# A two-layer graph network on one Trainium2 core: the last pair's first tile is summed on VectorE too, in a buffer of its own, with a new order of the last steps

## The chip, the cores and the metric

The kernel runs on one core of a Trainium2 chip. The metric is the device time of one execution in microseconds (us). TensorE is called PE here, VectorE DVE, ScalarE ACT, GpSimd POOL and SyncE SP; SP does nothing but issue DMAs.

## The reference, cut to what matters

The input x holds 128 graphs of 64 nodes with 768 features (8192 rows, fp32), adj their 64 x 64 adjacency. Two layers follow each other; each one is a layer norm, a relu, a graph layer and a residual sum. Layer 0 is a convolution over the relations of the edges. Layer 1 is an attention over each graph with 6 heads of 128 features. For one graph, in short:

```python
h1 = relu(layernorm(hh))                 # hh = x + layer 0
H  = h1 @ W + b                          # 64 x 768: six heads of 128
G  = h1 @ H_w + H_b                      # the gate's input, 64 x 768
t  = tanh(H)
l[i, j, head] = leaky(t[i] . w_src + t[j] . w_dst)   # masked by adj
A  = softmax(l over j)                   # 64 x 64 for each head
f  = elu(A @ H + b)                      # 64 x 768
out = hh + sigmoid(G) * (f - h1) + h1    # gate between f and h1, then the residual
```

The kernel uses tanh for the sigmoid: sigmoid(G) = (1 + tanh(G / 2)) / 2.

## The kernel before, in words

**Tiles and passes.** Two graphs make a tile of 128 rows: NT = 64 tiles, taken in NP = 32 pairs. Pass 1 (to L1038) computes layer 0 and writes hh + h1 into the output tensor in DRAM, and the operands of layer 1 into DRAM scratch. Pass 2 (L1041 on) computes layer 1 pair by pair and adds its result to the output tensor. This text is about the last some 50 us of pass 2.

**The products.** H and G of a pair come from 15 products of block sums (PRODUCTS, L54). The steps P, R, RA and Ff issue a product (L1121), its reading into the tiles `hz` by DVE or ACT, and an operand sum on POOL or DVE. In the last pair a product is split into its H half and its G half (PH and PG, `whole_product`, L1377), read by RH, RAH (ACT) and RG (`read_one`, L1388).

**One tile's attention.** With the names that the order uses:

- `th` (tanh, ACT, L1159), `mul` (DVE, L1163), four `sum` steps (twelve accumulating ACT operations, L1173), `k` and `chain` (POOL, L1176 to L1186), `rows` (PE, L1206), `rrow` (DVE, L1210) and `lrow` (ACT, L1215), `log` (PE, L1225), `cp` (masking, DVE, L1229), `pre` (leaky, ACT, L1234), `tr` (largest of a row, DVE, L1238), `exp` (six ACT operations, L1246), `rec` (1 / sum, DVE, L1250).
- The weights are turned for PE. All pairs but the last do it by `tv` (DVE, L1267), `ts` (four stores to DRAM, L1272) and `tl` (a load of 192 KB into `pT`, L1278). The last pair does it by `turnp` (PE, L1256) and `pT` (ACT, L1261).
- `swap` (L1192): two DMAs that put one graph's features on the other graph's partitions, into `hx`, of which there are two buffers. `att` (PE, L1286) needs pT, hz and hx.
- `ev` (`divide`, DVE, three operations each for an even and an odd half of the heads, L1322) writes the result `f`. `e` (ACT, L1333) is its exponential, `g` (ACT, L1329) the gate, `lx` (SP, L1061) the load of h1, scaled in pass 1.
- `f` (`final`, DVE, three operations of 128 x 768, L1340, L1342, L1344), then `dma` (`store`, L1347): a DMA issued by POOL that adds 384 KB of f to the output tensor.

**The last pair's end.** Here e, f and the stores are split by the parity of the heads: `exp_part` (L1417), `final_part` (L1422, L1424, L1426, L1428) and `store_part` (L1430). Tiles in SUMMED_HERE get their old output loaded beside their h1 (`load_out`, L1409, 384 KB, tile `xo`), the sum is a fourth DVE operation (L1428), and SP stores the half plainly (L1433). Other tiles are added to the output by POOL (L1435).

**What sets the order.** The steps of pass 2 are written out by hand: ORDER, which a loop runs for each pair (L1466), and END (L115 to L147, run from L1473) for the last pairs. "name/k" is the step of the k-th pair before the last; without "/k" it is the last pair's; the digit behind a name is the tile in its pair (0 or 1), and the digits behind points are parts. Every engine runs its own instructions in this order (`manual_schedule`, L1458), so an instruction that waits holds up all behind it on its engine. I write f0.2/1 for the step so named, and NT-2 and NT-1 for the last pair's tiles 0 and 1.

**Buffers.** `f` comes from the pool `work` with two buffers, so tile t waits for the store of tile t-2. `xo` comes from the pool `keep`, tag "x", six buffers.

**Fillers.** For tile NT-1 alone `keep_awake` (L1194) issues 9 matmuls ahead of `rows` and 12 ahead of `log` whose result is overwritten (L1198).

Of the kernel before, what the change touches and what calls it, by code (L numbers as in the profile page):

```python
# [8 lines left out]
F32 = mybir.dt.float32  # L9
# [6 lines left out]
P = 128  # L16
# [96 lines left out]


END = """  # L115
g0/3 R1/2 R2/2 R14/3 Ff6/2 P3.1/2 Ff1/1 P11.0/2 R3/2 RA1/2 P4.0/2 rows0/3 P4.1/2 tv1/4 P6.0/2 th1/3
Ff11/2 rrow0/3 R4/2 lrow0/3 mul1/3 Ff4/1 sum1.2/3 P6.1/2 lx0/4 dma0/5 P7.0/2 rec0/4 sum1.1/3
sum1.0/3 P7.1/2 P8.0/2 log0/3 R6/2 Ff2/1 Ff8/1 Ff3/1 Ff7/1 Ff9/1 ts1/4 R7/2 swap0/4 P8.1/2 P9.0/2
k1/3 sum1.3/3 tl1/4 RA7/2 P9.1/2 Ff5/1 chain1/3 P11.1/2 R8/2 g1/3 P10.0/2 rows1/3 cp0/3 Ff10/1
pre0/3 P10.1/2 lrow1/3 R9/2 tr0/3 R11/2 memset1/3 th0/2 tl0/4 rrow1/3 att/4 log1/3 P12.0/2 P12.1/2  # L120
R10/2 P13.0/2 lx1/4 P13.1/2 mul0/2 exp0.0/3 ev1.0/4 ev1.1/4 sum0.3/2 ev0.0/4 ev0.1/4 e1/4 e0/4
sum0.2/2 P5.0/1 memset0/2 R12/2 g0/2 f1.0/4 cp1/3 P2.0/1 g1/4 P0.0/1 exp0.1/3 Ff6/1 swap1/3 f1.1/4
P14.0/2 P0.1/1 R13/2 pre1/3 f0.0/4 P14.1/2 sum0.0/2 f1.2/4 P1.0/1 f0.1/4 P2.1/1 R0/1 sum0.1/2 f0.2/4
RA0/1 RA2/1 R14/2 P1.1/1 RA1/1 P5.1/1 ld/1 P3.0/1 Ff11/1 R2/1 tr1/3 RA14/2 R1/1 RA5/1 R5/1 th1/2
tv0/3 mul1/2 exp1.0/3 P3.1/1 P8.0/1 Ff1 P8.1/1 exp1.1/3 k0/2 P4.0/1 dma0/4 chain0/2 tv1/3 ts0/3
sum1.1/2 rows0/2 rrow0/2 R3/1 sum1.2/2 lx1/3 P4.1/1 Ff2 Ff4 P11.0/1 lrow0/2 Ff5 P6.0/1 sum1.0/2
sum1.3/2 log0/2 P6.1/1 R4/1 k1/2 P7.0/1 cp0/2 Ff8 pre0/2 R6/1 P7.1/1 tr0/2 P9.0/1 exp0.0/2 ts1/3
R8/1 dma1/4 Ff3 P9.1/1 memset1/2 Ff9 rec0/3 R7/1 Ff10 Ff7 exp0.1/2 tv0/2 chain1/2 tl0/3 rows1/2
RA7/1 lrow1/2 P11.1/1 rrow1/2 lx0/3 P10.0/1 log1/2 swap0/3 tl1/3 R9/1 rec1/3 P10.1/1 R11/1 cp1/2
R10/1 th0/1 att/3 pre1/2 P13.0/1 mul0/1 sum0.3/1 ev1.1/3 ev0.0/3 memset0/1 sum0.1/1 sum0.2/1  # L130
sum0.0/1 lx0/2 ev1.0/3 ts0/2 ev0.1/3 P13.1/1 k0/1 P12.0/1 P12.1/1 tr1/2 chain0/1 R13/1 swap1/2 PH2
swap0/2 e1/3 R12/1 e0/3 PH0 P14.0/1 P14.1/1 f1.0/3 f0.0/3 f1.1/3 exp1.0/2 R14/1 exp1.1/2 tv1/2 PH5
f1.2/3 rows0/1 f0.1/3 RA14/1 lrow0/1 RAH0 dma1/3 f0.2/3 PH1 PG0 PH3 ts1/2 th1/1 RAH5 RAH1 RAH2
mul1/1 PH11 dma0/3 tl0/2 PH4 RH3 lx1/2 memset1/1 Ff6 sum1.0/1 RH4 Ff11 tl1/2 sum1.1/1 PH6 rrow0/1
PH7 RH6 sum1.3/1 RAH7 log0/1 PH9 RG0 sum1.2/1 cp0/1 RH9 pre0/1 rec0/2 RH11 PH8 RH8 PH10 th0 k1/1
chain1/1 rows1/1 att/2 lrow1/1 tr0/1 exp0.0/1 exp0.1/1 rec1/2 RH10 mul0 rrow1/1 PH13 log1/1 ev0.0/2
ev0.1/2 tv0/1 PH12 sum0.3 ev1.1/2 cp1/1 lx0/1 sum0.2 e0/2 sum0.0 pre1/1 RH12 ts0/1 f0.0/2 PG2 PH14
sum0.1 k0 RG2 PG3 RH13 tr1/1 PG1 PG8 swap0/1 exp1.0/1 ev1.0/2 f0.1/2 exp1.1/1 chain0 tl0/1 RAH14 RG3
rec0/1 rows0 PG6 f0.2/2 RG1 memset0 th1 swap1/1 tv1/1 e1/2 mul1 f1.0/2 rec1/1 lx0 f1.1/2 lrow0 PG4
g1/2 att0/1 rrow0 sum1.1 PG5 log0 dma0/2 f1.2/2 ev0.0/1 sum1.0 sum1.2 memset1 RG6 cp0 sum1.3 pre0  # L140
ts1/1 lx1/1 tl1/1 RG4 k1 chain1 rows1 ev0.1/1 e0/1 RG5 tr0 PG7 rrow1 lrow1 f0.0/1 g0/1 RG7 log1
f0.1/1 swap0 att1/1 PG11 cp1 exp0.0 f0.2/1 dma1/2 ev1.0/1 PG9 exp0.1 ev1.1/1 RG9 g1/1 swap1 pre1
turnp0 dma0/1 e1/1 tr1 PG10 PG12 RG10 f1.0/1 rec0 pT0 att0 f1.1/1 f1.2/1 exp1.0 RG12 PG14 RG8 exp1.1
ev0.1 turnp1 e0.1 rec1 PG13 ev0.0 f0.0.1 e0.0 RG14 RG11 RG13 pT1 f0.1.1 f0.0.0 g0 dma1/1 att1 f0.2.1
f0.1.0 lx1 ev1.1 g1 ev1.0 e1.1 f1.0.1 e1.0 f1.1.1 f1.0.0 f1.2.1 f1.1.0 f1.3.1 f1.2.0 f1.3.0 f0.2.0
out1.1 out0.1 out1.0 out0.0
""".split()  # L147


# [1 line left out]
def kernel(  # L151
# [46 lines left out]
    G, N, D = x.shape  # L198
# [7 lines left out]
    NT = T // P  # L206
# [24 lines left out]
    keep = ctx.enter_context(tc.tile_pool(name="keep", bufs=1))  # L231
# [165 lines left out]
    with ExitStack() as px:  # L397
        wa = px.enter_context(tc.tile_pool(name="wa", bufs=1))
        work = px.enter_context(tc.tile_pool(name="work0", bufs=2))
# [61 lines left out]
        R2 = NROW - 2 * Q  # L461
# [579 lines left out]
    with ExitStack() as px:  # L1041
        wb = px.enter_context(tc.tile_pool(name="wb", bufs=1))
        work = px.enter_context(tc.tile_pool(name="work1", bufs=2))
# [111 lines left out]
        TH, PR, SD, SG, PS, AM, AL, PB, DN, MX, PT, PO, FF, EE, HX, TP = ({} for _ in range(16))  # L1155
# [160 lines left out]
        def divide(t, r):  # L1316

            if t not in FF:
                FF[t] = work.tile([P, D], F32, name="f")
            for c in range(HH):  # L1320
                h = 2 * c + r
                nc.vector.scalar_tensor_tensor(  # L1322
                    FF[t][:, h * DO : (h + 1) * DO], PO[t][r][c], DN[t][:, h : h + 1], bb,
                    op0=OP.mult, op1=OP.add)
# [21 lines left out]
        def store(t):  # L1346
# [8 lines left out]
            "dma": store,  # L1355
        }
        OF_TILE_PART = {"sum": sums, "exp": exps, "ev": divide, "f": final}

        def step(n, p):
# [43 lines left out]
        def part(v, r):  # L1403

            return v.rearrange("p (c r o) -> p r c o", c=HH, r=2)[:, r]
# [3 lines left out]
        def load_out(t):  # L1409
            if t in SUMMED_HERE:  # L1410
                XO[t] = keep.tile([P, D], F32, name="xo", tag="x", bufs=6)
                nc.sync.dma_start(XO[t], of[t * P : (t + 1) * P, :])
# [17 lines left out]
        def store_part(t, r):  # L1430
            to = part(of[t * P : (t + 1) * P, :], r)
            if t in SUMMED_HERE:
                nc.sync.dma_start(to, part(FF[t], r))  # L1433
# [21 lines left out]
        def parsed(order):  # L1455
            return [(n, int(k or 0)) for n, _, k in (x.partition("/") for x in order)]
# [5 lines left out]
        ends = [[last[f"e{n}{k}"] for n in g] for k in range(2)  # L1462
                for g in (("dev",), ("norm", "sum", "put"), ("turn", "tput"))]
        order = parsed(ORDER)
        SUMMED_HERE = (NT - 1,)
        for i in range(min(k for _, k in order), NP - 2):  # L1466
            for j, (n, k) in enumerate(order):
                if i * len(order) + j in FINISH:
# [54 lines left out]
```

## Time and profile before

| what | value |
|---|---|
| median of 3 runs (lowest, highest) | 2344.8 us (2343.53, 2345.41) |
| the profiled execution's own time | 2344.68 us |
| its span, first to last instruction | 2342.8 us |
| busy: PE, DVE, ACT, POOL | 99%, 83%, 55%, 19% |
| last DVE operation of the kernel ends | 2335.44 us |
| last DMA issue (POOL, L1435) | 2335.74 to 2336.89 us |

The profile counts from the first instruction. Its busy shares are means over the whole span; the last stretch differs from the rest, so times there are read from the timeline, which lists each instruction with its start, its length and, in brackets, how long its engine idled before it and what ended that. All times like "at 2317.13" are on this clock.

### The profile page before, as it was taken

The page shows a single profiled execution, that of the slowest core. Times are in us where ns is not written, and L with a number is a line of the kernel's source. Part 1 is how long each engine was busy: PE and PEld are TensorE (multiplying, and loading weights), DVE is VectorE, ACT ScalarE, POOL GpSimd, SP SyncE. Part 2 cuts the span into 40 slices and gives each one's busy share as a digit, 9 for nine tenths or more (in the row PEclk, how much of TensorE's full clock was granted, in tenths as well). Part 3 has the DMA queues.
Part 4 walks back from the last instruction along what each step waited for, and adds up shares of the span by engine and source line. Part 5 has one row for each costly group of instructions (what it writes and reads, how often), then busy time and mean ns, then how long its engine had stood idle before and what let it go on. Part 6 is the DMA issues. An engine that isn't in the chain of part 4 may idle for free.

```text
span 2342.8 us, 35503 instructions
## 1 busy us (share of the span) xinstructions
PE 2310.5 (99%) x11441; PEld 1645.8 (70%) x11441; DVE 1953.3 (83%) x3736; ACT 1280.8 (55%) x3843; POOL 439.6 (19%) x1099
## 2 busy tenths in 40 slices
PE   9999999999999999999999999999999999999995
PEld 7888888888888888888888884444444444444444
DVE  8877777777787777777777777899999999999997
ACT  2454454454543544544544524777667777777775
POOL 1111111111111111111111101122222222222222
PEclk9999999999999999999999999999999999999998
DMA  5335535435446445345355366667777776676766
GB/s 189 91 98 130 136 100 139 123 100 149 113 107 157 105 110 154 98 120 145 99 130 133 100 177 138 124 141 149 148 145 150 141 147 140 138 146 140 144 134 139
DMA packets 804983, 308.50 MB, mean 132 GB/s; under 512 B 622660, under 2 KB 755127, under 8 KB 804796
## 3 DMA queue, kind: packets, MB, share of 16 engines
q1 hardware_dynamic: 794924, 281.41, 50.4%
q0 software_dynamic: 9728, 24.78, 6.1%
q8 instruction: 90, 1.47, 0.3%
q14 instruction: 97, 0.79, 0.1%
q10 hardware_dynamic: 144, 0.04, 0.0%
HBM read 139.71 MB, written 140.87 MB: 120 GB/s over the span
## 4 chain that ended last, share of the span: by engine, by line
PE 95%; DMA 2%; DVE 1%; issue 1%; ACT 1%; SPq 0%; POOL 0%; POOLq 0%; DVEq 0%; ACTq 0%
PE pwa L814 21%; PE pwb L814 18%; PE pwcd L814 14%; PE pma L1121 14%; PE pmb L1121 11%; PE pmd L1121 5%; PE pmc L1121 5%; PE pb L742 3%; PE ps L1286 1%; PE pwcd L798 1%; PE pwcd L742 1%; PE ps L1225 1%; PE pmc L1286 0%; DVE weights L347 0%; DMA weights<-in_wself_t_dram 0%
## 5 line engine op out<-in xcount | busy, mean ns | idle before, releaser
L814 PE MATMUL pwa<-weights,op 128*128 128x256 f32 x2304 | 529.6, 379 | 0.3 <-DVE x L806 0.3
L814 PEld LDWEIGHTS pwa<-weights,op 128*128 128x128 f32 x2304 | 427.5, 190 | 56.0 <-issue 1.1
L814 PE MATMUL pwb<-weights,op 128*128 128x256 f32 x1932 | 451.3, 381 | 0.0
L814 PEld LDWEIGHTS pwb<-weights,op 128*128 128x128 f32 x1932 | 361.9, 190 | 51.4 <-issue 0.8
L347 DVE TENSOR_TENSOR op<-op 128x768 f32<-128x768 f32 x310 | 290.5, 946 | 94.5 <-ACT op L752 91.6
L814 PE MATMUL pwcd<-weights,op 128*128 128x256 f32 x1560 | 357.8, 379 | 0.0
L814 PEld LDWEIGHTS pwcd<-weights,op 128*128 128x128 f32 x1560 | 296.1, 190 | 40.1
L1121 PE MATMUL pma<-weights,op_f 128*128 128x512 f32 x620 | 291.2, 592 | 0.0
L1173 ACT ACTIVATE pr<-pr 128x128 f32<-128x128 f32 x768 | 225.5, 294 | 91.8 <-DVE pr L1163 91.7
L752 ACT COPY op<-pb 128x512 f32<-128x512 f32 (+1 forms) x132 | 70.8, 618 | 355.2 <-PE pb L742 355.2
L1121 PEld LDWEIGHTS pma<-weights,op_f 128*128 128x128 f32 x620 | 117.7, 190 | 147.4 <-issue 138.8
L324 POOL TENSOR_SCALAR rn<-su 128x1 f32<-128x1 f32 x124 | 24.8, 200 | 847.0 <-ACT hf L319 528.6
L1121 PE MATMUL pmb<-weights,op_f 128*128 128x512 f32 x372 | 180.9, 594 | 0.0
L547 ACT ACTIVATE hp<-x,rn 128x768 f32<-128x768 f32 x60 | 109.3, 1821 | 108.7 <-POOL rn L326 108.7
L1173 ACT ACTIVATION_READ_ACCUMULATOR pr<-pr 128x1 f32 x768 | 143.4, 187 | 0.0
L318 ACT ACTIVATE hf<-x 128x768 f32<-128x768 f32 x64 | 53.7, 839 | 149.1 <-DVE x L850 148.9
L1246 ACT ACTIVATE pb<-al,mx 128x64 f32<-128x64 f32 x384 | 128.1, 337 | 12.2 <-DVE mx L1238 12.1
L1347 POOL DMA_DIRECT2D out_dram<-f x62 | 55.0, 886 | 388.7 <-DVE f L1344 381.3
L1121 PEld LDWEIGHTS pmb<-weights,op_f 128*128 128x128 f32 x372 | 68.4, 190 | 84.0 <-issue 75.8
L1121 PE MATMUL pmb<-weights,h 128*128 128x512 f32 x248 | 122.5, 596 | 0.0
L1121 PE MATMUL pmc<-weights,op_f 128*128 128x512 f32 x248 | 121.8, 592 | 0.0
L806 DVE TENSOR_TENSOR x<-pwcd,x 128x256 f32<-128x256 f32 x127 | 53.4, 420 | 81.6 <-PE pwcd L798 81.5
(241 smaller groups left out, 4124.7 us busy)
## 6 DMA issues: line engine op xcount, KB each, us to landing
x<-in_x_dram SPq DMA_DIRECT2D x64, 384.0 KB
h<-ht SPq DMA_DIRECT2D x64, 384.0 KB
out_dram<-x SPq DMA_DIRECT2D x64, 384.0 KB
hh<-hh SPq DMA_DIRECT2D x64, 384.0 KB
h<-h SPq DMA_DIRECT2D x256, 96.0 KB
x<-hh SPq DMA_DIRECT2D x64, 384.0 KB
out_dram<-f POOLq DMA_DIRECT2D x62, 384.0 KB, 6.4
h<-hpt SPq DMA_DIRECT2D x60, 384.0 KB
```

Source lines behind the costliest of these rows:

```text
L318: nc.scalar.activation(by, src, AF.Copy, scale=-1.0 / D, accum_out=sums[:, 0:1])
L324: nc.gpsimd.tensor_scalar(to[:, 0:1], sums[:, 1:2], 1.0 / D, EPS, op0=OP.mult, op1=OP.add)
L347: return (nc.vector.tensor_add if s1 == "+" else nc.vector.tensor_sub)(to, x, y)
L547: nc.scalar.activation(hp.rearrange("p (b f i) -> p b f i", b=KB, f=NQ), X[t].rearrange("p (b i f) -> p b f i", b=KB, f=NQ), AF.Relu, scal ...
L742: nc.tensor.matmul(to[:, g, :, i, :], H0[2 * p + k][o, kb * P : (kb + 1) * P], rts[p % 2][o, k, :n].rearrange("p s n -> p (s n)"), start=T ...
L752: nc.scalar.copy(a[:, :n].rearrange("p s h (g n) -> p g (s h) n", g=GT), ps[:, :, c * n * KQ * N : (c + 1) * n * KQ * N].rearrange("p g (x ...
L806: nc.vector.tensor_add(v, bank[b][:, :CQ], v)
L814: nc.tensor.matmul(bank[b][:, :CQ], OPS[p, an][:, s, q, :], bw[bn][:, (s * KQ + q) * CQ : (s * KQ + q + 1) * CQ], start=(first and q == s ...
L1121: nc.tensor.matmul(bank[p, b], operand(p, an)[:, q, :], bw2[bn][:, 2 * q * CQ : 2 * (q + 1) * CQ], start=(first and q == 0), stop=(q == KQ ...
L1173: nc.scalar.activation(PR[t][:, j, h, :], PR[t][:, j, h, :], AF.Copy, accum_out=to)
L1246: nc.scalar.activation(PB[t][:, h, :], AL[t][:, h, :], AF.Exp, bias=MX[t][:, h : h + 1], accum_out=DN[t][:, h : h + 1])
L1347: nc.gpsimd.dma_start(of[t * P : (t + 1) * P, :], FF[t], accum_op=OP.add)
```

## The change

Three edits. First, SUMMED_HERE also holds tile NT-2: its old output is loaded, its sum is made on DVE in two halves, and both halves are stored plainly by SP, in place of two accumulating DMAs by POOL. Second, the result f of tile NT-2 takes a buffer of the pool `keep`, tag "x", in place of one of the two buffers of `work`. Third, END is written anew: 464 steps in place of 462, the same ones and f0.3.0 and f0.3.1, the two new sums. PE's matmuls are the same in number and form.

The core of the diff; of END, the lines that the last 45 us run:

```diff
 END = """
...
-sum0.1 k0 RG2 PG3 RH13 tr1/1 PG1 PG8 swap0/1 exp1.0/1 ev1.0/2 f0.1/2 exp1.1/1 chain0 tl0/1 RAH14 RG3
-rec0/1 rows0 PG6 f0.2/2 RG1 memset0 th1 swap1/1 tv1/1 e1/2 mul1 f1.0/2 rec1/1 lx0 f1.1/2 lrow0 PG4
-g1/2 att0/1 rrow0 sum1.1 PG5 log0 dma0/2 f1.2/2 ev0.0/1 sum1.0 sum1.2 memset1 RG6 cp0 sum1.3 pre0
-ts1/1 lx1/1 tl1/1 RG4 k1 chain1 rows1 ev0.1/1 e0/1 RG5 tr0 PG7 rrow1 lrow1 f0.0/1 g0/1 RG7 log1
-f0.1/1 swap0 att1/1 PG11 cp1 exp0.0 f0.2/1 dma1/2 ev1.0/1 PG9 exp0.1 ev1.1/1 RG9 g1/1 swap1 pre1
-turnp0 dma0/1 e1/1 tr1 PG10 PG12 RG10 f1.0/1 rec0 pT0 att0 f1.1/1 f1.2/1 exp1.0 RG12 PG14 RG8 exp1.1
-ev0.1 turnp1 e0.1 rec1 PG13 ev0.0 f0.0.1 e0.0 RG14 RG11 RG13 pT1 f0.1.1 f0.0.0 g0 dma1/1 att1 f0.2.1
-f0.1.0 lx1 ev1.1 g1 ev1.0 e1.1 f1.0.1 e1.0 f1.1.1 f1.0.0 f1.2.1 f1.1.0 f1.3.1 f1.2.0 f1.3.0 f0.2.0
-out1.1 out0.1 out1.0 out0.0
+RH13 ev0.0/2 log1/1 RH12 sum0.2 ev1.0/2 sum0.0 sum0.3 cp1/1 ev1.1/2 e0/2 pre1/1 lx0/1 PH14 swap0/1
+f0.0/2 g1/1 ts0/1 tr1/1 PG2 RAH14 f0.1/2 RG2 k0 f0.2/2 chain0 e1/2 PG1 RG1 PG8 RG3 f1.0/2 PG4
+exp1.0/1 PG5 exp1.1/1 dma0/2 rows0 th1 tv1/1 lrow0 swap0 RG4 f1.1/2 PG6 mul1 memset0 tl0/1 f1.2/2
+sum1.1 RG6 rrow0 att0/1 rec0/1 PG7 PG9 log0 RG7 PG10 sum1.0 RG5 dma1/2 sum1.2 ev0.0/1 sum1.3 PG11
+cp0 ts1/1 swap1/1 ev0.1/1 k1 pre0 tl1/1 RG9 chain1 tr0 e0/1 rows1 rec1/1 RG11 lrow1 f0.0/1 att1/1
+exp0.0 lx0 rrow1 exp0.1 log1 f0.1/1 ev1.0/1 ev1.1/1 RG8 memset1 cp1 e1/1 turnp0 lx1/1 RG10 PG12 pT0
+f1.0/1 rec0 pre1 f1.1/1 f1.2/1 att0 tr1 RG12 g0 PG14 exp1.0 ev0.0 PG13 ev0.1 e0.0 swap1 exp1.1 lx1
+turnp1 dma1/1 f0.0.0 e0.1 f0.2/1 f0.1.0 f0.0.1 f0.2.0 RG13 f0.3.0 f0.1.1 rec1 out0.0 RG14 f0.2.1 pT1
+att1 ev1.1 e1.1 ev1.0 g1 f1.0.1 dma0/1 e1.0 f0.3.1 f1.1.1 f1.0.0 out0.1 f1.2.1 f1.1.0 f1.3.1 f1.2.0
+f1.3.0 out1.1 out1.0
 """.split()
...
             if t not in FF:
-                FF[t] = work.tile([P, D], F32, name="f")
+                FF[t] = (keep.tile([P, D], F32, name="f", tag="x", bufs=6) if t == NT - 2 else
+                         work.tile([P, D], F32, name="f"))
...
-        SUMMED_HERE = (NT - 1,)
+        SUMMED_HERE = (NT - 2, NT - 1)
```

More of the change, by code (lines that the diff above doesn't have):

```diff
@@ L115 @@
 END = """
[L116 to L137, printed above, removed]
-sum0.1 k0 RG2 PG3 RH13 tr1/1 PG1 PG8 swap0/1 exp1.0/1 ev1.0/2 f0.1/2 exp1.1/1 chain0 tl0/1 RAH14 RG3
@@ L145 @@
-f0.1.0 lx1 ev1.1 g1 ev1.0 e1.1 f1.0.1 e1.0 f1.1.1 f1.0.0 f1.2.1 f1.1.0 f1.3.1 f1.2.0 f1.3.0 f0.2.0
-out1.1 out0.1 out1.0 out0.0
+P3.1/2 P11.0/2 RA1/2 Ff6/2 swap0/4 R2/2 R1/2 P4.0/2 R14/3 Ff1/1 rows0/3 Ff11/2 tv1/4 P4.1/2 Ff4/1
+memset1/3 R3/2 rrow0/3 g0/3 tl0/4 th1/3 P8.0/2 lrow0/3 Ff2/1 P6.0/2 R4/2 P6.1/2 Ff3/1 log0/3 P7.0/2
+P8.1/2 mul1/3 cp0/3 R6/2 pre0/3 sum1.2/3 ts1/4 Ff8/1 P7.1/2 Ff7/1 R7/2 tr0/3 rec0/4 RA7/2 Ff9/1
+P9.0/2 P9.1/2 P11.1/2 tl1/4 Ff5/1 sum1.0/3 R9/2 R8/2 sum1.1/3 P10.0/2 R11/2 P10.1/2 sum1.3/3 th0/2
@@ new lines @@
+Ff6/1 Ff10/1 R10/2 att/4 P13.0/2 lx0/4 mul0/2 dma0/5 exp0.0/3 g1/3 ev1.0/4 g0/2 ev0.1/4 ev1.1/4
+ev0.0/4 sum0.2/2 k1/3 g1/4 P13.1/2 P0.0/1 chain1/3 P12.0/2 P5.0/1 memset1/2 rows1/3 R13/2 rrow1/3
+P2.0/1 e1/4 P1.0/1 e0/4 lx1/4 f1.0/4 f0.0/4 P12.1/2 f1.1/4 sum0.0/2 P2.1/1 lrow1/3 R12/2 ld/1 P5.1/1
+log1/3 P0.1/1 f0.1/4 f1.2/4 exp0.1/3 sum0.3/2 P14.0/2 f0.2/4 R5/1 P14.1/2 sum0.1/2 RA0/1 P1.1/1 R0/1
+P3.0/1 k0/2 cp1/3 RA2/1 R14/2 RA1/1 Ff11/1 R1/1 P3.1/1 RA14/2 tv0/3 pre1/3 chain0/2 tr1/3 lx0/3 R2/1
@@ new lines @@
+th1/2 rows0/2 mul1/2 P4.0/1 P8.0/1 lrow0/2 exp1.0/3 R3/1 rrow0/2 exp1.1/3 P8.1/1 tv1/3 P4.1/1 Ff1
+sum1.2/2 memset0/2 lx1/3 R4/1 RA5/1 Ff2 Ff4 sum1.0/2 sum1.1/2 log0/2 Ff7 P6.0/1 P6.1/1 R6/1 Ff3
+cp0/2 swap1/3 sum1.3/2 P7.0/1 k1/2 P7.1/1 P9.0/1 RA7/1 P9.1/1 R8/1 swap0/3 chain1/2 Ff8 pre0/2
+rows1/2 ts0/3 P11.0/1 ts1/3 tr0/2 P11.1/1 tl1/3 lrow1/2 rec1/3 Ff9 exp0.0/2 rec0/3 R7/1 P10.0/1
+exp0.1/2 rrow1/2 R9/1 Ff10 R11/1 dma0/4 log1/2 tv0/2 cp1/2 P10.1/1 R10/1 tl0/3 P12.0/1 P12.1/1 att/3
+dma1/4 th0/1 pre1/2 P13.0/1 mul0/1 tr1/2 g0/1 R12/1 g1/2 sum0.0/1 sum0.1/1 P14.0/1 ev0.1/3 ev1.1/3
@@ new lines @@
+ev1.0/3 ev0.0/3 sum0.3/1 k0/1 sum0.2/1 e1/3 P13.1/1 e0/3 swap1/2 R13/1 f1.0/3 PH0 P14.1/1 swap0/2
+f0.0/3 f1.1/3 RA14/1 PH2 exp1.0/2 R14/1 chain0/1 PH1 f1.2/3 PH5 exp1.1/2 RAH0 tv1/2 memset0/1 f0.1/3
+rows0/1 f0.2/3 lrow0/1 th1/1 ts0/2 mul1/1 PH3 RAH5 PH11 RAH2 tl0/2 RAH1 PG0 RH3 PH4 Ff5 RH4 PH6 Ff6
+dma0/3 sum1.0/1 PH7 sum1.2/1 rrow0/1 sum1.1/1 RH6 rec0/2 RAH7 log0/1 PH9 dma1/3 Ff11 lx0/2 cp0/1
+sum1.3/1 k1/1 PH8 RG0 RH9 RH11 PH10 pre0/1 RH8 PH12 chain1/1 rows1/1 tr0/1 ts1/2 th0 RH10 lx1/2
+rec1/2 tl1/2 mul0 memset1/1 rrow1/1 att/2 exp0.0/1 exp0.1/1 sum0.1 lrow1/1 PH13 PG3 tv0/1 ev0.1/2
```

## The prediction

> **What bounds the kernel now.** I read the page first, for shares, then a table of windows over the last 140 us, then the list of waits there, then the timeline row by row. A difference of 0.2% (4.7 us) is about what a measurement of this kernel can tell from no change. The page says PE, until the last slice (tenths of busy time in 40 slices):
>
> ```profile
> PE   9999999999999999999999999999999999999995
> DVE  8877777777787777777777777899999999999997
> ```
>
> Pass 2 is the right third: DVE there is as full as PE. The change touches only the last 115 us (DVE's order first differs near 2228), so the table by stretch matters (busy PE, PEld, DVE, ACT, POOL, then granted clock, DMA share, GB/s):
>
> ```profile
> 2205.00:2255.00 50.00, 50.00 (x210) 23.09 (x209) 48.60 (x103) 36.83 (x158) 10.93 (x26) 1.00 0.56 109
> 2255.00:2290.28 35.28, 33.30 (x150) 19.64 (x148) 33.68 (x72) 26.02 (x127) 8.42 (x29) 1.00 0.78 165
> 2290.28:2300.00 9.72, 8.47 (x78) 6.74 (x77) 9.61 (x23) 8.80 (x50) 2.01 (x7) 1.00 0.48 125
> 2300.00:2307.00 7.00, 4.76 (x39) 2.89 (x38) 6.82 (x11) 6.83 (x31) 2.85 (x4) 1.00 1.02 213
> 2307.00:2316.00 9.00, 7.78 (x54) 4.84 (x55) 7.45 (x17) 5.77 (x21) 1.92 (x6) 0.81 0.64 152
> 2316.00:2320.00 4.00, 4.00 (x42) 3.30 (x40) 3.91 (x13) 2.49 (x9) 0.88 (x1) 1.00 0.80 194
> 2320.00:2329.35 9.35, 3.54 (x46) 2.46 (x35) 7.46 (x20) 4.35 (x13) 0.97 (x2) 0.97 0.68 130
> 2329.35:2335.50 6.15, 0.00 (x0) 0.00 (x0) 6.03 (x16) 1.23 (x2) 1.09 (x1) 0.50 0.36 43
> ```
>
> From 2290.28 (`mul` of NT-2) to the last DVE operation at 2335.44, DVE is busy 41.3 of 45.2 us, PE 28.6 of 45.2. So **DVE bounds the tail**: what it idles there, some 3.8 us, and the 7.36 us from its last operation to the end are all that a new order can win, with 3.0 us idle in 2205 to 2290. The timeline's brackets name the idle pieces:
>
> ```profile
> 2307.30 0.87 DVE L1322 SCALAR_TENSOR_TENSOR f<-ps,dn,bb 128x128 f32<-128x128 f32 x3 [0.47 <-DMA out_dram<-f]
> 2311.42 0.55 DVE L1210 TENSOR_TENSOR rrow<-ps,de 64x384 bf16<-64x384 f32 x1 [0.56 <-PE ps L1206]
> 2314.73 0.59 DVE L1229 COPY_PREDICATED a<-ai,ps 128x384 f32<-128x384 int32 x1 [0.70 <-PE ps L1225]
> 2317.13 0.88 POOL L1347 DMA_DIRECT2D out_dram<-f  x1 [7.06 <-DVE f L1344]
> 2324.39 0.87 DVE L1322 SCALAR_TENSOR_TENSOR f<-ps,dn,bb 128x128 f32<-128x128 f32 x3 [1.85 <-DMA out_dram<-f]
> 2327.16 0.32 PE L1286 MATMUL ps<-weights,pT 64*64 64x128 f32 x1 [2.58 <-ACT pT L1261]
> ...
> 2334.89 0.55 DVE L1426 SCALAR_TENSOR_TENSOR f<-weights,f 128x384 f32<-128x384 f32 x1
> 2335.74 1.15 POOL L1435 DMA_DIRECT2D out_dram<-f  x1 [5.30 <-DVE f L1426]
> ```
>
> The largest, 1.85: NT-2's `ev0.1` waits for the buffer of tile NT-4, whose store POOL issued at 2317.13 to 2318.01; it landed some 6.3 us later. att0 had ended at 2320.24. The wait spreads: `e0` on ACT follows `ev0`, `pT1` stands behind `e0` on ACT, att1 needs pT1, so PE stops too (2.58). The last rows are the end: DVE done at 2335.44, POOL issues to 2336.89, its DMA lands near 2340.5, the span ends at 2342.8.
>
> **The change, part by part.**
>
> *Buffer of its own.* In the listing of the changed program NT-2's first result operation waits for PE alone: its 1.85 goes, and pT1 and att1 come earlier with it. What is late next: NT-1's `ev1.1`, as before, waits for tile NT-3's store (dma1/1). That was issued at 2322.16, 0.29 after its f1.2/1, and landed 5.5 us after the issue ended.
>
> *Order.* The 0.47 goes: in the new order the store it waits for (tile NT-6's) is issued well ahead. The 0.56 and 0.70 (PE's rows and logits late for DVE) mostly go, as other DVE work now stands ahead of rrow1 and cp1. Between 2255 and 2290.28 DVE idled 1.60: 0.85 at 2271.99, at `ev` behind att/3, which PE had late, the rest in pieces of 0.3 and less. In the new order a product of the last pair stands where PE stopped. The gain upstream lies between 0 and 1.6; I take 1.0, the large piece and a little of the rest, so `mul0` at 2289.3.
>
> *DVE from mul0 to ev1.* Counted in the changed listing, with the pitch of each form in these rows (start to start): 12 operations of 768 columns at 0.87, 30 of L1322 at 0.26, 16 reads of 256 at 0.33, 7 of 384 at 0.47, 2 `mul` at 1.65, 3 each of rrow, cp and tr at 0.47, 0.49, 0.50, 2 `tv` at 0.5, 4 reciprocals at 0.12: 10.44 + 7.80 + 5.28 + 3.29 + 3.30 + 4.38 + 1.00 + 0.48 = **36.0 us**. Before, the same stretch took 39.07 (2290.28 to 2329.35), of it 3.8 idle. Without idle ev1 starts at 2289.3 + 36.0 = 2325.3; with all of the old idle at 2329.1. I take 1.1 of idle, what is left of the two PE waits and their links: **2326.4**. dma1/1 must have landed: from its end to ev1 the listing has 19 operations, 7.3 us by the same pitches, so f1.2/1 ends near 2319.0; POOL issues from 2319.3 to 2320.2 (0.88), landing 5.5 to 6.3 later, 2325.7 to 2326.5. Just in time.
>
> *Sums on DVE.* Two operations of 128 x 384 (L1428): 2 x 0.47 = +0.94, the bound engine's, so nothing hides them; they are in the counts. From ev1 on there are six of L1322 and nine of 384 columns both before and after: 6.1 us (2329.35 to 2335.44). DVE ends at **2332.5**, 2.95 earlier.
>
> *The last store.* Before, two DMAs followed DVE's end: the POOL add is issued 0.30 after it and ends the span 7.36 after DVE. Afterwards f1.3.0 is the last operation and SP stores plainly. The row of the SP store before:
>
> ```profile
> 2333.94 1.64 SPq L1433 DMA_DIRECT2D out_dram<-f  x2
> ```
>
> The second of the two issued at 2335.00; its data ended 2.1 us later. With a landing of 3.0 us from the issue (`ts` stores landed 1.9 to 3.6 after theirs) and the 2.3 that the span ran on after the last landing, the end is 5.3 after DVE, 5.4 with the link. So **-2.0**. From both sides: a landing 1.9 after issue gives -3.1, 3.6 gives -1.4. I take 3.0, between the data's end and the late bound.
>
> The Trainium skill speaks against a part of this: "DMA: Bandwidth & Descriptors", Anatomy of one DMA, puts most of a DMA's fixed 2 us into the receipt from the target memory, which a plain store to DRAM pays as an accumulating one does. In the trace the POOL DMA's data ended at 2339.0 and it landed at 2340.5, 1.5 of receipt, which agrees. By that rule the plain store lands 2.1 + 1.5 = 3.6 after its issue, and the sum loses 0.6.
>
> *POOL.* Loses two DMA issues (1.19 and 1.15), which nothing waits for but the end. dma0/1 goes to its last place; nothing waits for its buffer any more, and it is issued well before the end in the walk (2327 or so, landing 6.3 later, 2334), inside the SP store's end.
>
> *SP.* It gets xo0 (384 KB) and two stores, and a new sequence: swap1/1 (tile NT-3) waits for att0/1 to free hx; tl1/1 stands behind it, then lx0, xo0, lx1/1. att1/1 needs tl1/1, and 12 fillers, log1 and so DVE's cp1 stand behind att1/1 on PE. By the engines' rows in the new order ts1/1 is out and tl1/1 issued near 2306.9; landing 4.5 later as tl0/1 did (issued 2298.05, its att at 2302.62) is 2311.4, and log1 and cp1 follow 3.7 later (att 1.0, fillers 2.1, log1 and links 0.6): 2315.1. By the DVE counts cp1 is reached near there too, so xo0 and the sequence cost nothing if tl1/1 takes 4.5. The ends: 0, and the rivals below.
>
> **Sum:** 2344.68 - 2.95 - 2.0 = **2339.7 us**, against the profiled execution; the median of the runs shown is 0.1 higher, which I leave out.
>
> **The rivals.**
>
> *Nothing to be told (within 0.2%).* tl1/1 lands as late as tile NT-5's load did, with a store and loads beside it:
>
> ```profile
> 2284.19 7.30 DMA pT<-pt
> ```
>
> 7.3 (its wait is the 0.9 of PE at `DMA pT<-pt`) instead of 4.5 puts att1/1, the fillers, log1 and cp1 2.8 later, and DVE, in order, passes nothing by cp1: 2339.7 + 2.8 = **2342.5**. The upstream gain staying out (+1.0) and the receipt (+0.6) reach the same class by themselves. For it: three loads of 384 KB are issued right behind tl1/1. Against: with tl0/1, smaller neighbours, it took 4.5.
>
> *Slower: the load chain.* One mechanism: tl0/1, att0/1, swap1/1, tl1/1, att1/1, fillers, log1, cp1. If tl1/1 shares the DMA engines evenly with lx0, xo0, lx1/1 and tile NT-5's store, 192 + 4 x 384 KB = 1.77 MB go at the 213 GB/s of 2300 to 2307 in 8.3 us; with 1.9 for start and landing (the shortest `ts`) that is 10.2, not 4.5: 5.7 later, **2345.4**. If tl0/1 ahead of it also takes 7.3, 2.8 more; and if PE then stands long enough for its clock to drop, the 12 fillers run at the 0.32 apart that the 9 had after 3.9 us without weight loads, not 0.175: 12 x 0.145 = 1.7. Together **2349.9**. It decides against the change from a tl1/1 that lands 5.0 late, and by over 0.2% from 9.7. Against it: SP issues its loads 0.5 apart, and tl0/1 with loads issued behind it took 4.5. The Trainium skill ("TensorE: Matmul & The Clock Gate", Part 1) gives about 3.4 us of idleness for the drop of the clock, and the trace's 0.81 with the 3.9 agrees; by it this rival pays the 1.7, and the forecast, whose PE also rests before rows1's nine fillers, pays no more than before.
>
> *The change doesn't do what it says.* The wait only moves, from ev0 on dma0/1 to ev1 on dma1/1. With a landing of 7.3 in place of 6.3 or less, ev1 starts at 2327.5 and the time is 1.1 more, 2340.8; with f1.2/1 late by the old idle too, **2342.4** (2.7 more). The listing shows the wait, so it is likely to bind by some tenths; I count it under no difference.
>
> **How the numbers follow.** Forecast, faster by over 0.2% (below 2340.1): 0.46. It lies 0.4 from that bound, so one small term (upstream gain out, 1.0; 7.3 at tl1/1, 2.8; the moved wait, 1.1) takes it into no difference: 0.40. Slower by over 0.2%, the long load chain or a like stop in the 115 us of new order: 0.14. The range goes from no idle at all before ev1 (-1.1), all upstream idle gone (-0.6), the early landing (-1.1) and 0.4 for the links of the end, 2336.5, to the load chain's first price with a store that lands late (+0.6), 2346.0. The forecast's own range is 2336.5 to 2341.
>
> **What would show it.** Right: ev0 of NT-2 without a DMA in its bracket, near 2321; ev1 near 2326.4; the last DVE operation near 2332.5, of L1428; an SP store as the last DMA and 5.4 us from there to the end. Wrong: a bracket over 1.5 us at cp1 with PE waiting for `DMA pT<-pt` at att1/1 (the load chain); ev1 waiting for `DMA out_dram<-f` past 2327; DVE's last operation past 2335; over 6 us from it to the end.

## The result, and the profile after

The changed kernel takes **2336.1 us** (median of 5 runs, 2335.46 to 2338.55), the kernel before 2344.8 (5 runs, 2343.53 to 2346.42): a ratio of 0.9964 with a 95% interval of 0.9952 to 0.9975, 8.7 us at the medians. The way was forecast, the size was not: the time lies 0.4 below the range's low end. The profiled execution took 2335.71 with a span of 2333.9, against 2344.68 and 2342.8 before. All differences below are between profiled executions unless a ratio or a median is named.

The table by stretch of the changed kernel's last part, its boundaries set at the same events (`mul0` at 2288.78, ev1 at 2324.65, the end of the last VectorE operation at 2330.62); the columns are those of the prediction's table:

```profile
2288.78:2300.00 11.22, 8.92 (x77) 6.18 (x76) 11.06 (x27) 11.15 (x55) 2.50 (x8) 1.00 0.59 151
2300.00:2307.00 7.00, 6.12 (x48) 4.59 (x48) 7.00 (x13) 3.55 (x21) 2.04 (x4) 1.00 0.79 143
2307.00:2316.00 9.00, 8.18 (x85) 5.54 (x83) 9.00 (x25) 7.12 (x26) 1.40 (x6) 1.00 1.01 289
2316.00:2324.65 8.65, 4.90 (x35) 3.72 (x35) 8.62 (x21) 3.86 (x16) 1.77 (x2) 0.80 0.66 116
2324.65:2330.62 5.97, 0.00 (x0) 0.00 (x0) 5.94 (x16) 1.85 (x3) 0.00 (x0) 0.53 0.36 92
2330.62:2333.90 3.28, 0.00 (x0) 0.00 (x0) 0.00 (x1) 0.00 (x0) 0.00 (x0) 0.50 0.41 120
```

Each engine's busy time stands ahead of its count of operations, DVE's third. It is 41.6 of 41.8 us from `mul0` to its last operation, 0.2 idle where the kernel before had 3.8. And the last row, from DVE's end to the span's end, is 3.28 us long where it was 7.36.

The timeline of the changed kernel at the places that the prediction named: ev0, ev1, DVE's last operation, and SP's four stores in one row, the last issued at 2330.7:

```profile
2318.22 1.64 DVE L1323 SCALAR_TENSOR_TENSOR f<-ps,dn,bb 128x128 f32<-128x128 f32 x6
2324.65 1.63 DVE L1323 SCALAR_TENSOR_TENSOR f<-ps,dn,bb 128x128 f32<-128x128 f32 x6
2330.06 0.56 DVE L1429 TENSOR_TENSOR f<-f,xo 128x384 f32<-128x384 f32 x1
2323.43 7.76 SPq L1434 DMA_DIRECT2D out_dram<-f  x4
```

Neither ev row has a bracket: DVE waited for no store.

The other half of the gain is in the list of waits of SP's queue, whose last instruction (L1519, L1520 after the change) waits for the DMAs and then for the other engines (PEq is PE's sequencer; each row gives the sum, the number and the longest of the waits). The kernel before:

```profile
SPq L1519 <- DMA out_dram<-f: 3.7, 1, 3.7
SPq L1519 <- PEq L1519: 2.7, 2, 2.2
```

The changed kernel:

```profile
SPq L1520 <- DMA out_dram<-f: 1.3, 2, 1.0
SPq L1520 <- PEq L1520: 0.6, 2, 0.5
```

Both waits shrink, the second from 2.7 to 0.6. The prediction had carried what follows the last landing over unchanged.

### The profile page after: what moved, and what is told of

It is laid out like the page before. It is cut to its first block, busy times and chain, and to the rows that moved or that the text cites. A ratio compares the mean times of both kernels' runs of the same rounds, so it can differ in the third digit from the quotient of the medians.

```text
span 2333.9 us, 35510 instructions
## 1 busy us (share of the span) xinstructions
PE 2308.5 (99%) x11441; PEld 1645.1 (70%) x11441; DVE 1952.9 (84%) x3738; ACT 1280.4 (55%) x3843; POOL 442.2 (19%) x1097
## 4 chain that ended last, share of the span: by engine, by line
PE 95%; DVE 3%; DMA 2%; issue 0%; SPq 0%; ACT 0%; DVEq 0%; ACTq 0%
PE pwa L814 21%; PE pwb L814 18%; PE pwcd L814 14%; PE pma L1121 14%; PE pmb L1121 11%; PE pmd L1121 5%; PE pmc L1121 5%; PE pb L742 3%; PE ps L1286 1%; PE pwcd L798 1%; PE pwcd L742 1%; PE ps L1225 1%; DMA weights<-in_wself_t_dram 1%; DMA weights<-in_wadj_t_dram 1%; PE pmc L1286 0%
```

## The experiments

The column "end" is the time from the end of VectorE's last operation to the end of the span. The ratios and their intervals are to runs of the kernel before on the same chip, whose medians were 2345.76 for e1 to e4, 2346.24 for e5 to e8 and 2344.7 for e9 to e12. e11 is the changed kernel once more, on the chip of e9 to e12; where a kernel of another chip is set against it, the difference by the ratios is given too.

| kernel | `mul0` | VectorE's end | end | span | median | ratio to before (95%) |
|---|---|---|---|---|---|---|
| before | 2290.28 | 2335.44 | 7.36 | 2342.8 | 2344.8 | |
| changed | 2288.78 | 2330.62 | 3.28 | 2333.9 | 2336.1 | 0.9964 (0.9952 to 0.9975) |
| e1 old order, plain stores | 2290.16 | 2339.04 | 3.26 | 2342.3 | 2343.95 | 0.9995 (0.9986 to 1.0004) |
| e2 old order, own buffer | 2289.96 | 2332.84 | 7.86 | 2340.7 | 2342.73 | 0.9992 (0.9984 to 1.0001) |
| e3 old order, last steps swapped | 2289.89 | 2332.52 | 3.48 | 2336.0 | 2341.61 | 0.9983 (0.9974 to 0.9992) |
| e4 new order, POOL adds NT-2 | 2289.26 | 2331.31 | 4.49 | 2335.8 | 2336.89 | 0.9965 (0.9952 to 0.9977) |
| e5 new order, shared buffer | 2288.78 | 2333.44 | 3.26 | 2336.7 | 2338.94 | 0.9970 (0.9958 to 0.9982) |
| e6 new order, loads first | 2288.79 | 2337.46 | 3.24 | 2340.7 | 2341.84 | 0.9981 (0.9972 to 0.9990) |
| e7 new order, sums on POOL | 2289.25 | 2331.76 | 3.24 | 2335.0 | 2336.81 | 0.9961 (0.9948 to 0.9973) |
| e8 old order, plain stores, own buffer | 2289.89 | 2336.99 | 3.31 | 2340.3 | 2342.49 | 0.9983 (0.9974 to 0.9992) |
| e9 changed, last half added by POOL | 2288.79 | 2330.96 | 7.54 | 2338.5 | 2340.69 | 0.9983 (0.9975 to 0.9992) |
| e10 changed, last half stored plainly by POOL | 2289.22 | 2330.82 | 6.18 | 2337.0 | 2338.78 | 0.9980 (0.9971 to 0.9988) |
| e11 changed, again | 2288.81 | 2330.40 | 3.30 | 2333.7 | 2336.31 | 0.9966 (0.9954 to 0.9978) |
| e12 new order, POOL adds NT-2 early | 2289.40 | 2331.38 | 3.52 | 2334.9 | 2336.20 | 0.9967 (0.9955 to 0.9980) |

The column "end" falls in two groups whatever the order: 3.2 to 3.5 when SP stores last with nothing of POOL's open, 6.2 to 7.9 when POOL does. e4 lies between.

**The three edits on the old order: e1, e2, e8.**

```diff
 e1
-SUMMED_HERE = (NT - 1,)
+SUMMED_HERE = (NT - 2, NT - 1)
-f0.2.1 f0.1.0 ... f1.3.0 f0.2.0
+f0.2.1 f0.3.1 f0.1.0 ... f1.3.0 f0.2.0 f0.3.0
 e2
-FF[t] = work.tile([P, D], F32, name="f")
+FF[t] = (keep.tile([P, D], F32, name="f", tag="x", bufs=6) if t == NT - 2 else
+         work.tile([P, D], F32, name="f"))
 e8: both
```

> The old order, with NT-2 summed on VectorE and stored plainly (f0.3.1 behind f0.2.1, f0.3.0 behind f0.2.0); no own buffer. Theory A (the end after the last VectorE operation is a property of who issues the last store: 7.4 us behind a POOL accumulate, 3.3 behind an SP store): VectorE ends 0.9 later than before for the two sums, the span ends 3.3 after that, -3.1 us against before, 2341.7. Theory B (my recorded sum: the span runs on 2.3 us after any landing, 5.4 in all): -1.0, 2343.8. Theory C (the order alone gave all): +0.9.

> The old order and old stores; only the first tile's result gets a buffer of its own. Theory A (the wait is one of two in a row: ev0's store wait of 1.85 goes, but ev1 still waits for dma1/1, which lands near 2328.5 whatever ev0 does): -0.8 us against before, 2344.0, and a wait of about 1 us on a DMA stands in front of ev1. Theory B (the wait was the only thing in the way): -1.9, 2342.9.

> The old order with both other edits: NT-2 summed and stored plainly, and its own buffer. Theory A (edits add up: no store wait at ev0, -1.9 to -2.6 at VectorE's end; +0.9 for two sums; the end 3.3 instead of 7.4 behind it): -5.5 against before, 2339.5; the new order's own share is then about 3 us. Theory B (the order is the cause of nearly all): -2 or less.

e1's end is 3.26: theory A is right on the end. But VectorE ends 3.6 later than before, not 0.9, so that nothing is left of it. The timeline of e1 shows the largest piece at ev0:

```profile
2326.80 0.35 DVE L1322 SCALAR_TENSOR_TENSOR f<-ps,dn,bb 128x128 f32<-128x128 f32 x1 [3.35 <-DMA out_dram<-f]
```

3.35 in place of 1.85. From issue to landing POOL's last two accumulates took 8.6 and 5.8 us there, 4.7 and 4.8 in the changed kernel.

e2 loses this wait, and nothing takes its place at ev1: theory B. VectorE ends 2.6 earlier. The ratio's interval reaches 1, so that the gain in time, some 2 us, is shown by the profile alone.

e8 has both edits and gains 3.8 at the medians, between theory A's 5.5 and theory B's 2. Against e2 its end is 4.6 shorter (3.31 against 7.86), but VectorE ends 4.2 later, of which the two sums are 0.94. What its VectorE waits for, from the timeline of e8:

```profile
2307.71 0.87 DVE L1323 SCALAR_TENSOR_TENSOR f<-ps,dn,bb 128x128 f32<-128x128 f32 x3 [1.33 <-DMA out_dram<-f]
2311.89 0.55 DVE L1210 TENSOR_TENSOR rrow<-ps,de 64x384 bf16<-64x384 f32 x1 [0.63 <-PE ps L1206]
2313.65 0.42 DVE L1400 TENSOR_TENSOR weights<-pmb,weights 128x256 f32<-128x256 f32 x1 [0.35 <-PE pmb L1385]
2316.33 0.59 DVE L1229 COPY_PREDICATED a<-ai,ps 128x384 f32<-128x384 int32 x1 [1.39 <-PE ps L1225]
2327.49 0.42 DVE L1400 TENSOR_TENSOR weights<-pmb,weights 128x256 f32<-128x256 f32 x1 [0.62 <-PE pmb L1385]
```

The first wait is one tile earlier than ev0, at ev0.0/1 for tile NT-6's store. It is 0.92 in e1 and 1.33 in e8, which both load xo0 at 2300 in the old order, just ahead of that store; it is 0.47, 0.41 and 0.17 in before, e2 and e3, which do not. So in the old order xo0's load goes with some 0.8 more wait there (these five profiles agree; no run moved that load alone), and in e8 the logits come later at cp1 behind it (1.39 against 0.70 before); that the one causes the other is not shown. In the new order xo0 is issued at 2306.6, behind tl1/1, and none of these rows has a bracket. VectorE's end is 6.4 earlier in the changed kernel than in e8, which has all but the order: **with the two other edits in place the order is the largest part of the gain**, 4.5 to 6.4 us (from the two ratios, whose intervals just meet, and from the profiles).

**Which store is last: e3, e9, e10.**

```diff
 e3, on the kernel before
-ev1.0 e1.1 f1.0.1 ... f1.3.0 f0.2.0 out1.1 out0.1 out1.0 out0.0
+ev1.0 f0.2.0 out0.1 out0.0 e1.1 f1.0.1 ... f1.3.0 out1.1 out1.0
 e9, on the changed kernel (and f1.3.0 left out of END)
-            if t in SUMMED_HERE:
+            if t in SUMMED_HERE and (t, r) != (NT - 1, 0):
                 nc.sync.dma_start(to, part(FF[t], r))
 e10, on the changed kernel
-                nc.sync.dma_start(to, part(FF[t], r))
+                (nc.gpsimd if (t, r) == (NT - 1, 0) else nc.sync).dma_start(to, part(FF[t], r))
```

> The old order, old stores and buffers; only f0.2.0, out0.1 and out0.0 are moved up behind ev1.0, so that POOL's last accumulate is issued some 3 us earlier and the SP store of NT-1 comes last. VectorE's work is the same. Theory A (what ends the span is which store is last): span end is the later of VectorE's end plus 3.3 (2338.8) and POOL's last issue plus about 6 (near 2339.6): -3.2 us, 2341.6. Theory B (2.3 us follow any landing): -2.0 at most, 2342.8.

> The changed kernel with its very last half (even heads of NT-1) added to the output by POOL as the last DMA, without its sum f1.3.0 on VectorE. Theory A (the end behind the last VectorE operation depends on who stores last: 7.4 to 7.9 behind a POOL accumulate, 3.3 behind an SP store): VectorE ends 0.6 earlier, the end is 4.1 to 4.6 longer: +3.5 to +4.0 against the changed kernel, 2339.6 to 2340.1. Theory B (my recorded split: 2.3 us follow any landing, the stores differ by some 2): +1.4, 2337.5.

> The changed kernel with only the issuer of its very last store changed: POOL instead of SP, a plain store of the same sum. Theory A1 (what is long behind POOL's DMA is POOL's queue, its descriptors and the closing of its DMA): +3 or more, 2339 or more. Theory A2 (it is the accumulation, the read of the old output and the add on the way): +0.5 to +1 for POOL's longer issue (1.15 against 0.55), 2336.6 to 2337.1.

e3 moves three steps and has an end of 3.48: nothing of NT-2 need be stored plainly, it is enough that POOL's adds are not last. At the medians it is 4.2 below before (theory A: 3.2). Its profiled execution, 2337.82, is the fastest of its 11, with no store wait at ev0, though up to there its program is that of before: that wait differs between executions of the same instructions.

e9 puts one POOL add at the end of the changed kernel: the end is 7.54, the median 4.4 above e11 (theory A: 3.5 to 4.0). e10 is the same without the accumulation. Its end is 6.18 and its median 2.5 above e11: a little short of theory A1 (+3 or more) and far from theory A2 (+0.5 to +1). The waits of SP's queue in e10:

```profile
SPq L1520 <- DMA out_dram<-f: 3.3, 1, 3.3
SPq L1520 <- PEq L1520: 2.6, 2, 2.1
```

The second wait is 2.6, as behind the accumulate (2.7), not 0.6. The last half microseconds with any DMA traffic (the last number is GB/s) are these, in order in the kernel before, in e10 and in the changed kernel:

```profile
2338.50:2339.00 0.50, 0.00 (x0) 0.00 (x0) 0.00 (x0) 0.00 (x0) 0.00 (x0) 0.50 0.95 115
2333.00:2333.50 0.50, 0.00 (x0) 0.00 (x0) 0.00 (x0) 0.00 (x0) 0.00 (x0) 0.50 0.16 49
2332.50:2333.00 0.50, 0.00 (x0) 0.00 (x0) 0.00 (x0) 0.00 (x0) 0.00 (x0) 0.50 0.10 28
```

So the data stops near 2339.0 before and near 2333.2 in e10, 3.8 us ahead of the span's end in both; behind SP's store (changed) near 2332.55, 1.35 ahead. So of the 4.1 us between the ends of 7.36 and 3.28, some 2.9 are for POOL as the issuer (6.18 against 3.28) and about 1.3 for the accumulation (7.54 against 6.18). What POOL does in that time no row says.

**Are the sums worth it: e4, e12, e7.**

```diff
 e4, on the changed kernel (and f0.3.0, f0.3.1 left out of END)
-SUMMED_HERE = (NT - 2, NT - 1)
+SUMMED_HERE = (NT - 1,)
 e12: e4 with
-f0.1/1 ev1.0/1 ev1.1/1 RG8 memset1 cp1
+f0.1/1 f0.2/1 memset1 dma0/1 ev1.0/1 ev1.1/1 RG8 cp1
 e7, on the changed kernel
-                nc.vector.tensor_add(f, f, part(XO[t], r))
+                (nc.vector if (t, r) == (NT - 1, 0) else nc.gpsimd).tensor_add(f, f, part(XO[t], r))
```

> The changed kernel (new order, own buffer) without the sums on VectorE for NT-2: POOL accumulates both halves as before. Theory A (VectorE is the bound without idle, and POOL's stores end well before the last SP store): the two sums' 0.94 us come off, 2335.2, 9.6 less than before. Theory B (the plain store of NT-2 is what shortens the end; with POOL's adds the span ends some 6 us after their last issue near 2326.4, or later if they queue behind dma0/1): 2336 to 2338.

> New order and own buffer, NT-2 added by POOL without its two sums on VectorE, and tile NT-4's last operation and store moved up behind f0.1/1, so that POOL's adds do not queue behind it. Theory A (in the kernel with POOL's adds the closing of POOL's last DMA, 3.8 after its data, hid the sums' gain): POOL's last issue ends near 2326.3, its closing near 2332.2, VectorE ends near 2330.3 and the SP store ends the span near 2333.6: 2335.5, the same as or slightly below the changed kernel. Theory B (VectorE's two sums fill gaps that stay otherwise, and POOL's DMAs land late anyway): 2336.5 or more.

> The changed kernel with three of its four sums (both of NT-2 and the odd half of NT-1) on POOL, which idles there, in place of VectorE. Theory A (VectorE has no idle time left, so each 0.47 us taken from it counts): VectorE ends 1.4 earlier, 2334.7. Theory B (the two engines slow each other, or POOL's sum and its store end last): 2336 or more.

Without the two sums VectorE was to end 0.94 earlier. From `mul1` (the second L1163) to its end it takes 27.9 in e4 and 28.2 in e12, 28.2 in the changed kernel: the sums fill places that stay empty otherwise. Behind ev1 in e4 the second operation on one half starts 0.59 after the first instead of 0.47, and the next one 0.64 after that, when ACT's exponential of the other half has ended; in the changed kernel a sum stands between the first two, and these operations start 0.47 apart. So the sums cost 0.3 at most by these profiles. e4's end is 4.49, POOL's adds closing behind SP's store; e12 issues them earlier and has 3.52. e4's 2336.89 is theory B's, and e12's 2336.20 lies between its two theories. The changed kernel, e4, e12 and e7 below have the same time within what the runs can tell: the plain store of NT-2 was not needed in the new order.

e7 was to take 1.4 from VectorE, but VectorE ends 1.1 later than in the changed kernel, of which 0.5 was there at `mul0` already. The timeline of e7 shows why:

```profile
2323.44 0.98 POOL L1429 TENSOR_TENSOR f<-f,xo 128x384 f32<-128x384 f32 x1 [3.29 <-DVE f L1427]
2323.60 1.24 DVE L1425 SCALAR_TENSOR_TENSOR f<-f,x 128x384 f32<-128x384 f32 x1
...
2325.63 1.63 DVE L1323 SCALAR_TENSOR_TENSOR f<-ps,dn,bb 128x128 f32<-128x128 f32 x6
2325.80 0.99 POOL L1429 TENSOR_TENSOR f<-f,xo 128x384 f32<-128x384 f32 x1 [0.54 <-DVE f L1427]
...
2329.51 1.24 POOL L1429 TENSOR_TENSOR f<-f,xo 128x384 f32<-128x384 f32 x1 [2.73 <-DVE f L1427]
2329.93 1.23 DVE L1427 SCALAR_TENSOR_TENSOR f<-weights,f 128x384 f32<-128x384 f32 x1
```

Two of the three POOL sums meet an operation of VectorE with two operands in SBUF, and that one takes 1.24 and 1.23 instead of 0.55: each time VectorE loses more than the 0.47 that the sum would have cost. The sum beside ev1, whose first operand is in PSUM, slows nothing (1.63 as in the changed kernel). The Trainium skill ("GPSIMD Engine Reference", Specifications) names the SBUF interfaces as shared with VectorE, with contention where VectorE's instruction has two SBUF inputs; these rows agree.

**Buffer and load chain in the new order: e5, e6.**

```diff
 e5, on the changed kernel
-FF[t] = (keep.tile([P, D], F32, name="f", tag="x", bufs=6) if t == NT - 2 else
-         work.tile([P, D], F32, name="f"))
+FF[t] = work.tile([P, D], F32, name="f")
-f0.1/1 ev1.0/1 ev1.1/1 RG8 memset1 cp1
+f0.1/1 f0.2/1 memset1 dma0/1 ev1.0/1 ev1.1/1 RG8 cp1
 e6, on the changed kernel
-pre0 tl1/1 ... exp0.0 lx0 rrow1 ... turnp0 lx1/1 RG10
+pre0 lx0 lx1/1 tl1/1 ... exp0.0 rrow1 ... turnp0 RG10
```

> The changed kernel without the buffer of its own: NT-2's result shares the two buffers again, and so that its wait comes early, f0.2/1 and dma0/1 (tile NT-4's last operation and store) are moved up right behind f0.1/1, memset1 ahead of them. Theory A (what matters is when the store of NT-4 is issued, the buffer is only one way to get rid of the wait): f0.2/1 ends near 2312.8, the store is issued to 2314 and lands 4 to 7 later, near or before ev0 at 2319: within 1 us of the changed kernel's 2336.1. Theory B (the buffer is needed for the gain): a DMA wait of 2 us or more in front of ev0, 2338 or more.

> The changed kernel with the loads lx0, xo0 and lx1/1 (3 x 384 KB) issued ahead of tl1/1 instead of behind it. Theory A (my recorded rival's chain is real, tl1/1 only has little slack: its wait at att1/1 was 0.4 us): tl1/1 lands 3 to 5 us later, att1/1, the fillers, log1 and cp1 follow, and the time is 3 to 5 more than the changed kernel's: 2339 to 2341. Theory B (the loads behind it share the DMA engines with it anyway, so their order says nothing): no change, 2336.

e5 stands between its theories, with 1.16 of DMA wait in front of ev0, as its timeline shows:

```profile
2321.34 1.64 DVE L1322 SCALAR_TENSOR_TENSOR f<-ps,dn,bb 128x128 f32<-128x128 f32 x6 [1.16 <-DMA out_dram<-f]
```

It is 2.6 above e11 at the medians and by the ratios 0.9 above e11 and 1.4 above the changed kernel, with intervals that overlap: the buffer seems worth one to three microseconds in the new order, which an early store did not quite replace.

e6 shows the recorded rival's chain at work. The changed kernel issues tl1/1 at 2305.61, and PE begins att1/1 4.3 us later without a wait:

```profile
2305.61 0.39 SPq L1278 DMA_DIRECT2D pT<-pt  x1
2309.94 0.32 PE L1286 MATMUL ps<-weights,pT 64*64 64x128 f32 x1
```

(The 0.4 of wait that e6's expectation names is at 2289.76, at att/2.) In e6 tl1/1 is issued 1.1 later, behind the three loads, and PE waits for it at att1/1, which begins 8.0 after the issue; then the 12 fillers, in the timeline of e6:

```profile
2306.70 0.37 SPq L1278 DMA_DIRECT2D pT<-pt  x1
2314.71 0.44 PE L1286 MATMUL ps<-weights,pT 64*64 64x128 f32 x1 [4.48 <-DMA pT<-pt]
2316.33 4.01 PE L1198 MATMUL ps<-de,idr 128*128 128x384 bf16 x12
```

The fillers took 2.11 before and in the changed kernel; the granted clock of 2316 to 2320 is 0.50 in e6. VectorE idles 4.10 behind att1/1 and 2.34 at cp1, and the time is 5.5 above e11 at the medians, 3.5 by the ratios, 7.0 in the profiled spans (recorded for the single late load: 5.7; for 12 slow fillers 1.7, here 1.9). That is theory A, at the upper end of its 3 to 5 or above it. The Trainium skill ("TensorE: Matmul & The Clock Gate", Part 1) gives half speed after about 3.4 us of idleness; 4.48 of idleness and a clock of 0.50 agree.

## Why the prediction was right in its direction and wrong in its size

The sum, term by term, in the profiled executions:

| term | recorded | measured | difference |
|---|---|---|---|
| `mul0`, the gain upstream | 2289.3 | 2288.78 | -0.5 |
| `mul0` to ev1 | 36.0 + 1.1 idle | 35.87 | -1.2 |
| ev1 to VectorE's end | 6.1 | 5.97 | -0.1 |
| VectorE's end to the span's end | 5.3 | 3.28 | -2.0 |
| outside the span | 1.88 | 1.81 | -0.1 |

**The failed step is the last store.** The prediction read "a landing of 3.0 us from the issue" and "the 2.3 that the span ran on after the last landing", -2.0 in all, with -3.1 as its outer bound; measured was -4.1. Two readings failed there. The time from issue to landing counts from the issue's start, so the last POOL add (3.6 from 2335.74) landed at 2339.3, and 3.5 us followed it, not 2.3; SP's own waits agree, with 3.7 for the DMA behind its last issue, which ended at 2335.58. And that remainder was taken for the program's when it is POOL's: it is there behind a plain POOL store too (e10), and gone behind SP's (e1, e3, e8). The clue was in the list of SP's waits of before, 3.7 for the DMA and then 2.7 more for the engines, which the prediction did not split. The rule of the Trainium skill that it weighed ("DMA: Bandwidth & Descriptors", Anatomy of one DMA: most of the fixed 2 us is the receipt) is stated there for GpSimd's DMAs; that an SP store pays it alike was the prediction's own step. The 1.5 of receipt read from the trace was the same misreading: from the end of the data near 2339.0 to the landing at 2339.3 it is some 0.3, which does not agree, and here the measurement decides. Behind SP's data a receipt can be at most a part of the 1.35.

**The idle time** was the second term. The count of 36.0 us of VectorE work between `mul0` and ev1 was right to 0.13; the 1.1 of idle put on top was not there. In e10 and e11, the same instructions up to ev1, the stretch took 35.6; in e9, the same again, it took 36.8 with 0.9 idle, so some executions do have it. dma1/1, which was to land "just in time" at 2325.7 or later, was early. The 5.5 us that the same store took in the kernel before count from the issue's start too, which is 0.9 less; the issue came 0.8 sooner than counted; and the landing took 4.7 from it:

```profile
2318.49 0.90 POOL L1348 DMA_DIRECT2D out_dram<-f  x1 [8.49 <-DVE weights L1402]
```

So it landed near 2323.2, 1.4 us ahead of ev1.

**Right:** VectorE as the bound of the tail; the waits that go, at ev0 and three smaller ones; no DMA in front of ev0 and ev1; the upstream gain within its bounds. It is 1.5 between these two profiles, but `mul0` starts at 2290.04 in the mean of the five profiles of the old order and at 2289.01 in that of the nine of the new one, 1.0 earlier, as taken: the -0.5 of the table's first row is within the scatter of single executions. The sums' 0.94 were in the count of operations, and e4 and e12 show that leaving them out gains 0.3 at most. **The rivals:** tl1/1 did not land late (PE began att1/1 4.3 us after its issue, without a wait), but e6 shows that an issue 1.1 us later, behind the loads, would have brought about the first price of the load chain. The credit was given wrongly in one point: the prediction spoke of the buffer and the store as the parts that gain and of the order as what clears small waits. e8 gains 3.8 with buffer and store; the order does the rest.

What stays open: why the store wait at ev0 is 0, 1.85 and 3.35 in three executions of the old order, and what the engines do for 2 us more behind POOL's last DMA.

## What to carry to other kernels

Let the last transfer of a program be one that is not issued by GpSimd, and read the end as issue, landing and the final wait for the engines, each from its own row. In a tail where one engine is full, count that engine's operations by their pitch and add no idle time unless a row names who will wait; then ask of each removed operation whether it only filled a gap. Put a load that a late chain needs ahead of loads that are merely due: issued 1.1 us later and behind three of them, one load reached PE 4.8 us later, which cost three to seven.

## What the runs showed of the hardware that was not expected

- Behind the last POOL DMA of this program the span goes on for 3.8 us after the data stops, accumulating (before) or not (e10); behind SP's last store for 1.35.
- POOL's accumulating stores of 384 KB landed 4.7 us after issue in the changed kernel and up to 8.6 in e1.
- A POOL sum of 128x384 (0.98 to 1.24 us) stretched VectorE operations on two SBUF operands from 0.55 to 1.24, and the one set beside it that read its first operand from PSUM (ev1 in e7) not at all.
